# Attention b: periods of a pair, all maxima products of a pair at once in row halves, six shared PSUM banks

## The chip, the cores and the metric

The kernel runs on one core of a Trainium2 chip. The metric is the device time of one execution in microseconds (us); the figure for a kernel is the median of several runs. Differences of under about 0.3% cannot be told from no change.

## What is computed

Two transformer layers on a batch of 2 sequences of 512 tokens, width 512. Each sub-layer is added to the residual stream `x` after a layer norm:

```
x = x + attn_a(ln(x))   # 32 heads of 128, 8 key heads, quantized weights, rope, causal softmax
x = x + ffn(ln(x))      # 8 low-rank experts, the best 2 of 8 by a softmax gate
x = x + attn_b(ln(x))   # 32 query heads of 16, 8 key heads, rope, causal softmax
x = x + ffn(ln(x))
```

The change lies in `attn_b`. For each query head, with q and k of 16 numbers and scale 1/4:

```
att  = einsum('bhgqd,bhkd->bhgqk', q, k) / sqrt(16), masked to k <= q
probs = softmax(att); ctx = einsum('bhgqk,bhkd->bhgqd', probs, v); out = ctx @ Wo
```

## The kernel before

Attention a and the first experts of sequence 0 fill the first part of the time. From about 809 us the kernel is in the loop of attention b, which works on 32 *pairs* (two query heads each, numbered p; `h` is the head in the pair). Two pairs that share a key group position make a *unit* of four heads.

A query or key has 16 numbers, each split in a high and a low part; four combinations of the parts stand in 64 rows (`HALF`), so that float32r products, which run in one pass, come out exact enough. The tiles `qs` (five in rotation, `NQ`) and `ks` have 128 rows: rows 0 to 63 hold the parts, rows 64 and 65 hold the negative row maximum in two parts (in `qs`) against -1 (in `ks`), the rest zeros.

Each pair goes through three kinds of work:

- `maxima` (L742): for the four row tiles of each head, a product of queries and keys into PSUM (`sc_b`, L758, 8 matmuls of 128, 256, 384 or 512 columns over all 128 rows), a masked maximum on VectorE (`DVE`, L762), and the maxima rounded in two parts into `mm` on GpSimd (`POOL`, L770 and L771). It yields three times: tiles 0 and 1, then 3, then 2, each group in two banks.
- `maxima_in` (L776): four transposes of `mm` on TensorE (`tpm`, L781), and two casts on ScalarE (`ACT`, L784) that put the maxima into `qs`.
- `probabilities` (L789): the products again, transposed and with the maximum already subtracted (`st_b`, L805, 8 matmuls in six banks, three yields of two banks), the exponential on ACT (`pT_b`, L811), and the causal cut of the diagonal tiles on POOL (L814). After the second pair of a unit, `weighted_b` (L824) multiplies the four heads' probabilities with the values into one bank (`num_b`, L831; four heads side by side in strips of 32 columns), which ACT copies out (L842). `divided` (L860) and `output_b` (L878) finish the heads.

PSUM has eight banks here: five in `ps_x` for `sc_b`, `st_b` and `tpm` in turn, one in `ps_n` for `num_b`, two in `ps_f` for the side work. The order on TensorE is written out by hand; the tile framework adds the waits. A loop over `total + LEAD` steps (`STEPS` is 3 steps for a pair, `LEAD` is 8) issues in each step one third of a pair's maxima, one third of the probabilities of an earlier pair, now and then `maxima_in`, values that are `due`, and *side work*: experts, the projections of sequence 1, and outputs, taken from generators at a `pace` of us per step. Queries are loaded by `queries_in` (L734), one DMA a pair on the SP queue; as rows 64 and 65 must be zero when the maxima are taken, POOL clears them for each reused tile (L740). `queries_halved` (L724) prepares four pairs at once.

Of the kernel before, what the change touches and what calls it, by code (L numbers as in the profile page):

```python
# [40 lines left out]
def kernel(  # L41
# [21 lines left out]
    nc = tc.nc  # L63
# [6 lines left out]
    x = {}  # L70
# [12 lines left out]
    tri = const.tile([P, S], F32, tag="tri", name="tri")  # L83
# [634 lines left out]
    def keys_in(b, kh):  # L718

        if kh == 0:  # L720
            kparts[b] = spread(khls[b], f"k_{b}", (slice(0, 4, 2), slice(1, 4, 2)))
        nc.sync.dma_start(ks[kh][:HALF], kparts[b][:, ts(kh, 4), :])

    def queries_halved(p):  # L724

        b, kh, g, _ = pairs[p]
        hl = hlp.tile([P, 2, S], F32R, tag="hl", name=f"hl_{p}")
        src = qTs[b][:, kh * 2 + g // 2, :]
        nc.scalar.copy(hl[:, 0, :], src)
        nc.gpsimd.tensor_tensor(hl[:, 1, :], src, hl[:, 0, :].bitcast(F32), ALU.subtract)  # L730
        to = spread(hl, f"q_{p}", (slice(0, 2), slice(2, 4)))
        for n in range(4):
            qparts[p + n] = to

    def queries_in(p):
        _, _, g, pr = pairs[p]
        q = qs[p % NQ]
        nc.sync.dma_start(q[:HALF], qparts.pop(p)[:, ts((g % 2) * 2 + pr, 2), :])
        if p >= NQ:
            nc.gpsimd.memset(q[HALF:HM], 0.0)  # L740

    def maxima():  # L742

        for p, (b, kh, g, pr) in enumerate(pairs):
            q, k = qs[p % NQ].bitcast(F32R), ks[kh].bitcast(F32R)
            top = small.tile([P, NT, 2], F32, tag="top", name=f"top_{p}")
            for tiles in ((0, 1), (3,), (2,)):
                sc = [
                    ps_x.tile([P, S], F32, tag="x", name=f"sc_b_{p}_{tiles[0]}_{h}")
                    for h in range(2)  # L750
                ]
                parts, at = [], 0
                for i in tiles:
                    n = (i + 1) * P
                    parts += [(i, n, h, sc[h][:, at : at + n]) for h in range(2)]
                    at += n
                for i, n, h, part in parts:
                    nc.tensor.matmul(  # L758
                        part, q[:, h, ts(i, P)], k[:, pr * 2 + h, :n], start=True, stop=True
                    )  # L760
                for i, n, h, part in parts:
                    nc.vector.tensor_tensor_reduce(  # L762
                        part, part, tri[:, S - n :], 1.0, -3e38, ALU.add, ALU.max,
                        top[:, i, h : h + 1],
                    )
                if tiles == (2,):
                    mm = mms[p] = mmp[p % len(mmp)]
                    for h in range(2):
                        at = (1 - h) * HALF
                        nc.gpsimd.tensor_copy(mm[:, :, at], top[:, :, h])  # L770
                        nc.gpsimd.tensor_tensor(  # L771
                            mm[:, :, at + 1], top[:, :, h], mm[:, :, at].bitcast(F32), ALU.subtract
                        )
                yield

    def maxima_in(p):  # L776

        mm = mms.pop(p).bitcast(F32)
        tp = ps_x.tile([P, S], F32, tag="x", name=f"tpm_{p}")
        for t in range(NT):  # L780
            nc.tensor.transpose(tp[:HM, ts(t, P)], mm[:, t, :], ident)  # L781
        for h in range(2):
            at = (1 - h) * HALF
            nc.scalar.copy(qs[p % NQ][HALF:HM, h, :].bitcast(F32R), tp[at : at + 2, :])  # L784


    due = []

    def probabilities():  # L789

        for p, (b, kh, g, pr) in enumerate(pairs):
            q, k = qs[p % NQ].bitcast(F32R), ks[kh].bitcast(F32R)
            for tiles in ((0,), (1,), (3, 2)):
                wide = sum(S - j * P for j in tiles)
                for h in range(2):
                    sp = pr * 2 + h
                    st = ps_x.tile([P, S], F32, tag="x", name=f"st_b_{p}_{tiles[0]}_{h}")
                    pT = ptp.tile(
                        [P, wide], F32, tag=f"pT{wide}", name=f"pT_b_{p}_{tiles[0]}_{h}",
                        bufs=5 if wide == S else 8,  # L800
                    )
                    at = 0
                    for j in tiles:
                        n = S - j * P
                        nc.tensor.matmul(  # L805
                            st[:, at : at + n], k[:, sp, ts(j, P)], q[:, h, j * P :],
                            start=True, stop=True,
                        )
                        pTs[b, kh, g, j, sp] = pT[:, at : at + n]
                        at += n  # L810
                    nc.scalar.activation(pT, st[:, :wide], AF.Exp)  # L811

                    diag = pT[:, : len(tiles) * P].rearrange("p (m n) -> p m n", n=P)
                    nc.gpsimd.affine_select(  # L814
                        diag, diag, [[0, len(tiles)], [1, P]], ALU.is_ge, 0.0,
                        base=0, channel_multiplier=-1,
                    )
                if pr == 1:
                    for j in sorted(tiles):
                        pT4 = [pTs.pop((b, kh, g, j, n)) for n in range(4)]  # L820
                        due.append((p * STEPS + LEAD + 2 * (j > 0) + (j > 1), (b, kh, g, j, pT4)))
                yield

    def weighted_b(b, kh, g, j, pT):  # L824
# [1 line left out]

        first, last = j == 0, j == NT - 1
        if first:
            nums[b, kh, g] = ps_n.tile([P, S], F32, tag="num", name=f"num_b_{b}_{kh}_{g}")
        for sp in range(4):  # L830
            nc.tensor.matmul(  # L831
                nums[b, kh, g][ts(sp, STRIP), j * P :], vpads[b][:, j, kh, sp, :], pT[sp],
# [78 lines left out]
    for kh in range(2):  # L911
        keys_in(0, kh)
    queries_halved(0)
    for p in range(2):
        queries_in(p)
    parts(later, 14)

    ms, ps = maxima(), probabilities()
    total = len(pairs) * STEPS
    half = total // 2  # L920
    banks[:] = BESIDE
    side = chain(later, projections(1))
    pace, left = 1.05, 0.0
    for step in range(total + LEAD):
        with tc.manual_schedule(engines={mybir.EngineType.PE}):
            if step == half - 8:
                run(side)
                keys_in(1, 0)
            if step == half - 4:
                side = output_b(0, (0, 1))  # L930
                pace, left = 0.38, 0.0
            if step == half + LEAD:
                keys_in(1, 1)
            if step == half + LEAD + 10:
                side = chain(side, output_b(0, (2, 3)), experts(0, "f2", True))
                pace, left = 1.05, 0.0
            if step == total - 6:
                side = chain(output_b(1, (0, 1)), side)
                pace, left = 1.5, 0.0
            quotients[:] = [q for q in quotients if next(q, None) is not None]  # L940
            p, at = divmod(step + 4, STEPS)
            if at == 0 and p % 4 == 3 and p + 1 < len(pairs):
                queries_halved(p + 1)
            if at == 0 and 2 <= p < len(pairs):
                queries_in(p)
            p, at = divmod(step - 4, STEPS)
            if at == 0 and 0 <= p < len(pairs):
                maxima_in(p)
            if LEAD <= step:
                next(ps)  # L950
            if step < total:
                next(ms)

            if len(due) > 1 and due[1][0] <= step:
                for _ in range(2):
                    weighted_b(*due.pop(0)[1])
            left += pace
            while left > 0:
                got = next(side, None)
                if got is None:  # L960
                    left = 0.0
                else:
                    left -= got
    banks[:] = ALONE
    while due:
        weighted_b(*due.pop(0)[1])
# [95 lines left out]
```

## Time and profile before

| what | us |
|---|---|
| median of 3 runs (1113.66 to 1117.13) | 1114.39 |
| the profiled execution's own time | 1118.06 |
| its span, first to last instruction | 1116.3 |
| loop of attention b, first `sc_b` to last `num_b` (809.4 to 1055.3) | 246 |
| of it with much side work (839.4 to 892.3), seven pairs | 52.9 |
| of it with little side work (892.3 to 959.0), ten pairs | 66.7 |
| after the loop, to the end | 61 |

The granted TensorE clock was 0.992 of full speed over the span. All durations of single instructions come from that one profiled execution. TensorE's instructions overlap in the profile, so that the time one of them takes is best read from the start of one to the start of the next. A float32 product appears as two matmuls, a float32r product as one.

### The profile page before, as it was taken

How to read it: one execution, taken by the hardware profiler on the slowest of the kernel's cores; microseconds unless marked ns; L12 is line 12 of the kernel's file. 1: busy time of each engine (PE TensorE's matmuls, PEld its weight loads, DVE VectorE, ACT ScalarE, POOL GpSimd, SP SyncE). 2: the span in 40 equal slices, each digit the busy share in tenths (PEclk: the TensorE clock that was granted, in tenths of full speed). 3: DMA queues.
4: the chain of work that ended last, by engine and by line, in shares of the span. 5: the costliest groups of instructions: out<-in, count | busy, mean ns of one | idle time of the engine just before them, and what ended most of it. 6: DMA issues, size and time to landing. Idle time of an engine off the chain costs nothing.

```text
span 1116.3 us, 16200 instructions
## 1 busy us (share of the span) xinstructions
PE 1060.7 (95%) x4940; PEld 708.8 (63%) x4940; DVE 880.8 (79%) x2195; ACT 617.4 (55%) x1421; POOL 587.4 (53%) x920
## 2 busy tenths in 40 slices
PE   5799999999999999999999999999989989999988
PEld 3467677777777777777777777546457555555543
DVE  6889899999999999999999889574376677877252
ACT  3556566577566566566565665513157566585410
POOL 2557566666656656756756666261245566454200
PEclk9999999999999999999999999999989999999999
DMA  7301011022010010010021000042342235111000
GB/s 288 114 1 38 1 38 38 1 76 68 9 39 24 15 38 14 26 38 8 32 76 38 1 1 1 1 156 63 91 156 77 61 106 152 44 44 26 10 33 38
DMA packets 21030, 58.11 MB, mean 52 GB/s; under 512 B 3152, under 2 KB 4112, under 8 KB 18128
## 3 DMA queue, kind: packets, MB, share of 16 engines
q1 hardware_dynamic: 20944, 57.08, 15.6%
q8 instruction: 40, 0.66, 0.2%
q14 instruction: 46, 0.38, 0.1%
HBM read 43.30 MB, written 12.58 MB: 50 GB/s over the span
## 4 chain that ended last, share of the span: by engine, by line
PE 80%; DVE 10%; ACT 3%; POOL 3%; issue 2%; DMA 1%; SPq 0%; ACTq 0%; DVEq 0%; POOLq 0%
PE av L429 11%; PE sc L396 11%; PE tp L424 5%; PE ps_o L439 5%; PE ps_o L438 5%; PE ps_q L358 5%; PE ph_f L207 5%; PE ps_q L359 5%; PE num_b L831 3%; PE st_b L805 3%; PE py_f L266 3%; PE sc_b L758 3%; PE pq_b L678 2%; PE po L885 2%; DVE r_q L365 2%
## 5 line engine op out<-in xcount | busy, mean ns | idle before, releaser
L404 ACT ACTIVATE p<-sc,nmx 128x128 f32<-128x128 f32 (+3 forms) x256 | 135.7, 530 | 95.1 <-DVE nmx L399 92.1
L376 POOL TENSOR_TENSOR r_q<-r_q,tab 128x512 f32<-128x512 f32 x64 | 82.5, 1289 | 190.2 <-DVE rs_q L375 190.2
L396 PE MATMUL sc<-kT,qT 128*128 128x128 f32 (+3 forms) x512 | 180.0, 433 | 1.2 <-POOL qT L377 0.9
L365 DVE SCALAR_TENSOR_TENSOR r_q<-ps_q,s_q,r_q 128x512 f32<-128x512 f32 x192 | 143.4, 747 | 36.1 <-PE ps_q L359 22.4
L413 POOL TENSOR_SCALAR p<-p,rden 128x128 f32<-128x128 f32 (+3 forms) x256 | 140.3, 562 | 58.5 <-DVE rden L411 24.5
L425 ACT COPY pT<-tp 128x128 f32<-128x128 f32 (+3 forms) x256 | 109.4, 428 | 104.1 <-PE tp L424 103.5
L762 DVE CUSTOM_DVE_ANT_0 sc_b<-sc_b,tri 128x128 f32<-128x128 f32 (+3 forms) x256 | 119.6, 516 | 47.3 <-PE sc_b L758 42.5
L429 PE MATMUL av<-pT,v 128*128 128x512 f32 (+3 forms) x512 | 148.5, 433 | 0.0
L429 PEld LDWEIGHTS av<-pT,v 128*128 128x128 f32 x512 | 97.0, 190 | 80.2 <-issue 53.9
L448 DVE SCALAR_TENSOR_TENSOR acc<-ps_o,s_o,acc 128x512 f32<-128x512 f32 x186 | 137.3, 738 | 5.5 <-PE ps_o L439 5.4
L399 DVE CUSTOM_DVE_ANT_0 sc<-sc,tri 128x128 f32<-128x128 f32 (+3 forms) x256 | 125.1, 489 | 8.1 <-PE sc L396 7.3
L358 PE MATMUL ps_q<-xh,w_q 128*128 128x512 f32 x256 | 122.7, 479 | 7.6 <-DVE r_q L365 7.6
L424 PE MATMUL tp<-ident,p 128*128 128x128 f32 x640 | 112.9, 272 | 2.6 <-POOL p L413 2.6
L396 PEld LDWEIGHTS sc<-kT,qT 128*128 128x128 f32 x512 | 95.6, 189 | 25.3 <-ACT p L404 2.0
L438 PE MATMUL ps_o<-ah,w_o 128*128 128x512 f32 x256 | 107.9, 422 | 1.7 <-DVE acc L448 1.0
L811 ACT ACTIVATE pT_b<-st_b 128x384 f32<-128x384 f32 (+1 forms) x192 | 90.1, 528 | 34.4 <-PE st_b L805 33.5
L439 PE MATMUL ps_o<-al,w_o 128*128 128x512 f32 x256 | 104.8, 410 | 3.5 <-DVE al L152 3.5
L424 PEld LDWEIGHTS tp<-ident,p 128*128 128x128 f32 x640 | 83.0, 141 | 30.7 <-issue 6.4
L359 PE MATMUL ps_q<-xl,w_q 128*128 128x512 f32 x256 | 101.2, 395 | 0.0
L814 POOL TENSOR_SCALAR_AFFINE_SELECT pT_b<-pT_b 128x128 f32<-128x128 f32 (+1 forms) x192 | 62.2, 333 | 64.7 <-ACT pT_b L811 62.2
L377 POOL TENSOR_TENSOR qT<-r_q,rs_q 128x512 f32<-128x512 f32 x64 | 85.5, 1335 | 1.0
L446 POOL TENSOR_TENSOR acc<-acc,part 128x512 f32<-128x512 f32 x62 | 79.9, 1288 | 10.2 <-ACT part L445 10.1
(182 smaller groups left out, 2065.4 us busy)
## 6 DMA issues: line engine op xcount, KB each, us to landing
codes_q<-in_q_codes_dram SPq DMA_DIRECT2D x8, 1024.0 KB
codes_o<-in_o_codes_dram SPq DMA_DIRECT2D x8, 1024.0 KB
spread_q<-hl SPq DMA_DIRECT2D x16, 512.0 KB
qs<-spread_q SPq DMA_DIRECT2D x32, 256.0 KB
x_a<-in_x_dram SPq DMA_DIRECT2D x8, 256.0 KB
codes_k<-in_k_codes_dram SPq DMA_DIRECT2D x2, 1024.0 KB
codes_v<-in_v_codes_dram SPq DMA_DIRECT2D x2, 1024.0 KB
x_r<-in_x_dram SPq DMA_DIRECT2D x8, 256.0 KB
```

The costliest lines, as they stand in the source:

```text
L358: nc.tensor.matmul(ps, w[:, c, ts(h, A_HD)], xh[b][:, c, :], start=True, stop=False)
L359: nc.tensor.matmul(ps, w[:, c, ts(h, A_HD)], xl[b][:, c, :], start=False, stop=True)
L365: nc.vector.scalar_tensor_tensor(r, ps, s, r, ALU.mult, ALU.add)
L396: nc.tensor.matmul(sc[:, :n], qT[:, ts(i, P)], kT[:, :n], start=True, stop=True)
L399: nc.vector.tensor_tensor_reduce(sc[:, :n], sc[:, :n], tri[:, S - n :], -(A_HD**-0.5), 3e38, ALU.add, ALU.min, nmx,)
L404: nc.scalar.activation(pr, sc[:, :n], AF.Exp, bias=nmx, scale=-1.0, accum_out=den[:, i % 2 : i % 2 + 1],)
L413: nc.gpsimd.tensor_scalar(prs[j], prs[j], rden[:, j % 2 : j % 2 + 1], 1.0, ALU.mult, ALU.mult)
L424: nc.tensor.transpose(tp[:, j, :], prs[i][:, ts(j, P)], ident)
L429: nc.tensor.matmul(av[:, j * P :], v[:, j, :], pT[:, j, j * P :], start=(j == 0), stop=(j == NT - 1))
L438: nc.tensor.matmul(ps, w[:, h, ts(n, P)], ah, start=True, stop=False)
L439: nc.tensor.matmul(ps, w[:, h, ts(n, P)], al, start=False, stop=True)
L448: nc.vector.scalar_tensor_tensor(to, ps, s, to, ALU.mult, ALU.add)
```

## The change

A pair's three steps become one *period*. In each period, in TensorE's order: values of a finished unit (all 16 products, four tiles by four heads, in one go), then all eight maxima products of pair n into six banks, then side work and the three parts of the probabilities of pair n-2 in turn, with `maxima_in` of pair n-1 ahead of the third part. The maxima products read 64 rows only: head 0 of a pair stands in rows 0 to 63, head 1 in rows 64 to 127, each with its maxima in the first two rows of the other half. POOL no longer clears rows; queries and keys come with two DMAs of half the size. The bank of `num_b` joins the others: six in one pool.

```diff
-        nc.gpsimd.memset(pad[HALF:HM], -1.0)
+        for sp in range(4):
+            at = (1 - sp % 2) * HALF
+            nc.gpsimd.memset(pad[at : at + 2, sp, :], -1.0)
...
-    ps_x = ctx.enter_context(tc.tile_pool(name="ps_x", bufs=5, space=PSUM))
-    ps_n = ctx.enter_context(tc.tile_pool(name="ps_n", bufs=1, space=PSUM))
+    ps_x = ctx.enter_context(tc.tile_pool(name="ps_x", bufs=6, space=PSUM))
...
-    STEPS, LEAD = 3, 8
+    LEAD = 2
...
-        nc.sync.dma_start(ks[kh][:HALF], kparts[b][:, ts(kh, 4), :])
+        for h in range(2):
+            nc.sync.dma_start(
+                ks[kh][ts(h, HALF), h : 4 : 2, :], kparts[b][:, kh * 4 + h : kh * 4 + 4 : 2, :]
+            )
...
-        q = qs[p % NQ]
-        nc.sync.dma_start(q[:HALF], qparts.pop(p)[:, ts((g % 2) * 2 + pr, 2), :])
-        if p >= NQ:
-            nc.gpsimd.memset(q[HALF:HM], 0.0)
+        of = qparts.pop(p)
+        for h in range(2):
+            nc.sync.dma_start(qs[p % NQ][ts(h, HALF), h, :], of[:, (g % 2) * 4 + pr * 2 + h, :])
...
+            two, three, one = (
+                [ps_x.tile([P, S], F32, tag="x", name=f"sc_b_{p}_{i}_{h}") for h in range(2)]
+                for i in (2, 3, 1)
+            )
+            parts = []
+            for i in (2, 0, 3, 1):
+                n = (i + 1) * P
+                for h in range(2):
+                    part = (two[h][:, 384:], one[h][:, :n], two[h][:, :n], three[h])[i]
+                    parts.append((i, n, h, part))
+                    rows = ts(h, HALF)
                     nc.tensor.matmul(
-                        part, q[:, h, ts(i, P)], k[:, pr * 2 + h, :n], start=True, stop=True
+                        part, q[rows, h, ts(i, P)], k[rows, pr * 2 + h, :n], start=True, stop=True
                     )
...
-                        due.append((p * STEPS + LEAD + 2 * (j > 0) + (j > 1), (b, kh, g, j, pT4)))
+                        due.append((p + LEAD + 1, (b, kh, g, j, pT4)))
...
-            nums[b, kh, g] = ps_n.tile([P, S], F32, tag="num", name=f"num_b_{b}_{kh}_{g}")
+            nums[b, kh, g] = ps_x.tile([P, S], F32, tag="x", name=f"num_b_{b}_{kh}_{g}")
...
-    pace, left = 1.05, 0.0
-    for step in range(total + LEAD):
+    pace, left = 3.2, 0.0
...
+    for n in range(total + LEAD + 1):
...
+            for _ in range(3):
+                quotients[:] = [q for q in quotients if next(q, None) is not None]
+            if n % 4 == 1 and n + 3 < total:
+                queries_halved(n + 3)
+            if 0 < n and n + 2 < total:
+                queries_in(n + 2)
+            fill(0.1)
...
+            while due and due[0][0] <= n:
+                weighted_b(*due.pop(0)[1])
+            if n < total:
                 next(ms)
+            for part in range(3):
+                fill((0.5, 0.2, 0.2)[part])
+                if part == 2 and 1 <= n <= total:
+                    maxima_in(n - 1)
+                if LEAD <= n < total + LEAD:
+                    next(ps)
```

`fill(share)` takes side work worth that share of the pace. The paces of the later stages become 1.2, 3.2 and 4.5 us a period where they were 0.38, 1.05 and 1.5 us a step, and the stages begin at the same pairs as before.

More of the change, by code (lines that the diff above doesn't have):

```diff
@@ L746, in maxima @@
             top = small.tile([P, NT, 2], F32, tag="top", name=f"top_{p}")
[L747 to L757, printed above, removed]
+            two, three, one = (
+                [ps_x.tile([P, S], F32, tag="x", name=f"sc_b_{p}_{i}_{h}") for h in range(2)]
+                for i in (2, 3, 1)
+            )
@@ L760, in maxima @@
                     )
[L761 to L773, printed above, removed]
@@ L774, in maxima @@
-                yield
+            for i, n, h, part in parts:
+                nc.vector.tensor_tensor_reduce(
+                    part, part, tri[:, S - n :], 1.0, -3e38, ALU.add, ALU.max, top[:, i, h : h + 1]
+                )
+            mm = mms[p] = mmp[p % len(mmp)]
+            for h in range(2):
+                at = (1 - h) * HALF
+                nc.gpsimd.tensor_copy(mm[:, :, at], top[:, :, h])
+                nc.gpsimd.tensor_tensor(
+                    mm[:, :, at + 1], top[:, :, h], mm[:, :, at].bitcast(F32), ALU.subtract
+                )
@@ L776, in maxima_in @@
+            yield
     def maxima_in(p):
@@ L782, in maxima_in @@
         for h in range(2):
-            at = (1 - h) * HALF
-            nc.scalar.copy(qs[p % NQ][HALF:HM, h, :].bitcast(F32R), tp[at : at + 2, :])
+            rows = slice((1 - h) * HALF, (1 - h) * HALF + 2)
+            nc.scalar.copy(qs[p % NQ][rows, h, :].bitcast(F32R), tp[rows, :])
     due = []
@@ L913 @@
     queries_halved(0)
-    for p in range(2):
+    for p in range(3):
         queries_in(p)
@@ L918 @@
     ms, ps = maxima(), probabilities()
-    total = len(pairs) * STEPS
+    total = len(pairs)
     half = total // 2
@@ L922, with fill @@
     side = chain(later, projections(1))
-    pace, left = 1.05, 0.0
-    for step in range(total + LEAD):
+    pace, left = 3.2, 0.0
+    def fill(share):
+        nonlocal left
+        left += pace * share
+        while left > 0:
+            got = next(side, None)
+            if got is None:
+                left = 0.0
+            else:
+                left -= got
+    for n in range(total + LEAD + 1):
         with tc.manual_schedule(engines={mybir.EngineType.PE}):
-            if step == half - 8:
+            if n == half - 3:
@@ L927 @@
                 run(side)
                 keys_in(1, 0)
-            if step == half - 4:
+            if n == half - 1:
                 side = output_b(0, (0, 1))
-                pace, left = 0.38, 0.0
-            if step == half + LEAD:
+                pace, left = 1.2, 0.0
+            if n == half + LEAD:
                 keys_in(1, 1)
-            if step == half + LEAD + 10:
+            if n == half + LEAD + 4:
                 side = chain(side, output_b(0, (2, 3)), experts(0, "f2", True))
-                pace, left = 1.05, 0.0
@@ L937 @@
-            if step == total - 6:
+                pace, left = 3.2, 0.0
+            if n == total - 2:
                 side = chain(output_b(1, (0, 1)), side)
[L939 to L951, printed above, removed]
-                next(ms)
[L954 to L963, printed above, removed]
+                pace, left = 4.5, 0.0
```

## The prediction, made before the change was run

> **What bounds the kernel now.** I read the page first, then the busy time by stage, then the timeline of the loop of attention b.
>
> ```profile
> span 1116.3 us, 16200 instructions
> ...
> PE 1060.7 (95%) x4940; PEld 708.8 (63%) x4940; DVE 880.8 (79%) x2195; ACT 617.4 (55%) x1421; POOL 587.4 (53%) x920
> ...
> PE av L429 11%; PE sc L396 11%; PE tp L424 5%; PE ps_o L439 5%; PE ps_o L438 5%; PE ps_q L358 5%; PE ph_f L207 5%; PE ps_q L359 5%; PE num_b L831 3%; PE st_b L805 3%; PE py_f L266 3%; PE sc_b L758 3%; PE pq_b L678 2%; PE po L885 2%; DVE r_q L365 2%
> ```
>
> TensorE is busy 95% of the span and carries 80% of the chain that ended last; but the lines of attention b (num_b, st_b, sc_b) are only 3% each, so a change there moves per cents at most. By stage:
>
> ```profile
> core 0: us, PE busy (x) PEld busy (x) DVE busy (x) ACT busy (x) POOL busy (x), PEclk, DMA share, GB/s
> ...
> 839.40:892.30 52.90, 52.20 (x314) 34.28 (x314) 35.76 (x139) 32.75 (x75) 30.37 (x85) 1.00 0.25 71
> 892.30:959.00 66.70, 58.89 (x386) 34.88 (x384) 50.39 (x181) 44.78 (x92) 41.45 (x113) 1.00 0.38 116
> ```
>
> In the first stretch (seven pairs, much side work, 7.55 us a pair) TensorE is busy 52.2 of 52.9 us and nothing else is near: it bounds. In the second (ten pairs, little side work, 6.67 us a pair) TensorE is busy 58.9 of 66.7 us and no engine is full: waits bound. In the timeline the time of TensorE's work is read from start to start:
>
> ```profile
> 859.74 0.51 PE L758 MATMUL sc_b<-ks,qs 128*128 128x384 f32 x2
> 860.09 1.02 PE L678 MATMUL pq_b<-wq,xnT_b 128*128 128x512 f32 x2
> ...
> 861.29 0.62 PE L758 MATMUL sc_b<-ks,qs 128*128 128x128 f32 x4
> 861.75 1.02 PE L678 MATMUL pq_b<-wq,xnT_b 128*128 128x512 f32 x2
> 862.61 0.60 PE L781 MATMUL tpm<-ident,mm 128*66 128x128 f32 x4
> 862.97 0.70 PE L805 MATMUL st_b<-qs,ks 128*128 128x128 f32 x4
> 863.51 0.63 PE L758 MATMUL sc_b<-ks,qs 128*128 128x512 f32 x2
> 864.07 1.71 PE L831 MATMUL num_b<-pT_b,vpad 128*32 128x512 f32 x16
> 865.71 1.12 PE L678 MATMUL pq_b<-wq,xnT_b 128*128 128x512 f32 x2
> ```
>
> The maxima's products of a pair (L758) take 0.35 us (384 columns twice), 0.46 (128 and 256 twice) and 0.47 (512 twice; the 0.56 shown to the values holds a switch): 1.28 us. The transposes tpm take 0.44 with their tail, a pair's L805 as much as its maxima, 1.28. The first half of a unit's values takes 1.64 us; the second, in the same view, 0.79 (867.58 to 868.37). As single matmuls of 512 columns there start every 0.43 us, four strips together, the eight passes should take 2.13: 0.15 us per group goes into entering and leaving the strips. A busy period is thus 1.28 + 1.28 + 0.44 + 2.43/2 + side work 3.13 = 7.34, against 7.55 measured; only 0.2 us a pair is waiting.
>
> What happens behind the third part of the probabilities is in the timeline of all engines:
>
> ```profile
> 914.62 0.63 PE L781 MATMUL tpm<-ident,mm 128*66 128x128 f32 x4
> ...
> 915.01 0.70 PE L805 MATMUL st_b<-qs,ks 128*128 128x128 f32 x4
> 915.29 1.17 ACT L784 CAST qs<-tpm 2x512 fp32r<-2x512 f32 x2 [0.48 <-PE tpm L781]
> ...
> 915.55 0.83 PE L758 MATMUL sc_b<-ks,qs 128*128 128x512 f32 x2
> ...
> 916.48 0.87 ACT L811 ACTIVATE pT_b<-st_b 128x384 f32<-128x384 f32 x2
> ...
> 917.10 0.77 POOL L814 TENSOR_SCALAR_AFFINE_SELECT pT_b<-pT_b 128x256 f32<-128x256 f32 x2 [0.32 <-ACT pT_b L811]
> ```
>
> E, the moment when TensorE is done with that part, is 915.55, where the next product starts. ACT has the two casts of the maxima in front of the exponentials, so these end at E+1.36 and E+1.80 (917.35), and POOL's cut of the second at E+2.32 (917.87). The waits over the loop:
>
> ```profile
> POOL qs L740 <- PE st_b L805: 25.3, 26, 1.8
> ...
> PEld tpm L781 <- POOL mm L771: 14.3, 16, 2.1
> ...
> PE tpm L781 <- POOL mm L771: 7.0, 8, 1.9
> ```
>
> TensorE waits 21 us for mm before the transposes, most of it with little side work; POOL's clearing stands in the same queue and itself waits 25 us for L805.
>
> **The change, part by part.** Products in row halves: a pair's 8 products of 1.28 us become four pairs of neighbours, each in its own half. No row of before is in row halves. Bounds: 1.28 us if the halves run one after another, 0.64 if they run together. The nearest row is the values' strips, where four matmuls start 7 ns apart; I take 0.64 and keep 1.28 for the range. Two more switches a pair at 0.075 each (half of the 0.15 above), but one group of values instead of two a unit, 0.15 back.
>
> A rule of the Trainium skill speaks against it: "TensorEngine Tiling (Array Packing)", PSUM Bottleneck, says that tiling speeds up TensorE and not the emptying of PSUM. Here the maxima's reductions start 0.24, 0.38, 0.49 and 0.62 us apart for the four widths (timeline at 906.5 to 912.3), 3.46 us a pair on DVE. By the rule the saved 0.64 would be lost in all 32 periods (plus 20 us against a sum that counts it). By the trace DVE was busy 35.8 of 52.9 us in the busy stretch, so it is won there and lost only where side work is scarce. I follow the trace.
>
> The border of two periods: this is the new wait. Six maxima banks of six can't be had until the probabilities' banks are empty. In turn, tile 2 and 0 take banks of the first and second part (free), tile 3 the second's and that of tpm, tile 1 the two of the third part, which ACT frees at E+1.4 and E+1.85. TensorE works in order, so everything written behind the eight products waits.
> - A period without values: 0.3 us of side work, products, wait for the last bank, last product: TensorE is free at E+2.05, where it would be at E+0.94. Then side work 2.83, L805 1.28, tpm 0.44: period 6.60.
> - A period with values: 0.3 side, the first two tiles' values 1.6 (E+1.9), then the wait for POOL's cut (E+2.4), 0.65 more, products; the last takes the bank of num_b, which ACT copies 0.35 us later in 0.6: TensorE is free at E+4.3, not E+3.2. With 4.55 behind it: 8.85.
> The mean is 7.73 against 7.55: +0.18 for some 15 busy periods (pairs 4 to 11, 22, 23 and 26 to 30), +2.7 us. The gain of 0.64 and of the waits for mm is there, but 1.1 us a period is waited.
>
> Little side work (ten periods): now the chain is DVE's. Without values: the first reduction starts at E+0.5 (0.3 from a product's start to DVE's, as at 911.37 and 911.74), 3.46 us of them free the last bank at E+4.1, and tpm's end and the third part's second half behind it set the next E at E+4.85. With values the products start at E+3.15 and everything is 3.2 later: E+8.05. Mean 6.45. Two sets of divisions fall here (reciprocals 2 x 1.74, shuffles 2 x 0.75, products 2 x 0.69 = 6.4 us of DVE each) and four additions of 0.68; the 3 us in which DVE now idles during the values take most, I charge 6 us. 64.5 + 6 = 70.5 against 66.7: +4 us. The waits for mm are gone in this figure, since tpm comes a period later.
>
> At nothing: POOL loses 27 clearings of 0.945 us (25.5 us and 25.3 waited), hidden before by ACT's exponentials, which POOL still waits for; if that cover were gone it would be a gain. SP issues 64 DMAs of queries for 32 (0.47 us each: +15 us on SP over the loop) and 8 for 4 of keys; SP is idle most of the time, and queries are now asked for two periods (13 us) ahead of use, before 1.33 pairs (9 us); the spread's DMAs in front of them in SP's queue still come a period earlier. If that cover failed, the products of a pair would be late by the difference. The eight short memsets of -1 replace two of 2.0 us at 747 us, 29 us ahead of the keys. Side work is the same in sum and in its stages, 35 periods for 34.7. The last values stand inside the loop with 4 us of side work behind them; the end from 1055 us on is left at 61 us.
>
> Sum: 2.7 + 4 = +6.7 us on a profiled execution of 1118.1 us, which is 3.7 above the median; on the median of 1114.4 I put +6: 1120.
>
> **The rivals.**
> - Faster: the border waits don't come, since ACT does the exponentials ahead of the casts, or the side work at the border covers them. For: ACT is busy under 70% of either stretch; its order isn't written by hand. Against: in the chain above the casts come first, being ready first. Then the busy periods are 7.73 - 1.1 + 0.3 = 6.9 (-0.65, times 15: -10), little side work about -3 (values' wait gone): -13, 1101.
> - Even: TensorE waits half of that at the border: busy periods 7.2 (-5), the rest +2 to +4: within 3 us of before, 1113.
> - Slower by one mechanism: the row halves do not run together, or each switch drains for as long as a product. Where values are due, 0.64 more per pair then lies on the path (without values it is hidden in the wait for the banks): 16 x 0.64 = +10 on top of +6: 1130. It decides from about 0.2 us per pair. For it: no row of before shows such a product, and a switch to strips costs. Against: the strips run together.
> - It does not do what it says: if all six banks at once make DVE the chain even in busy periods (the skill's rule), the lead of DVE there, 1.7 us by my times (tpm's bank is free at E+4.0 and asked for at E+5.7), must be gone; side work on DVE of more than that in a period does it. +20 - 6 of the waits it covers: about 1134.
>
> **How the numbers follow.** Forecast (+2 to +12) 0.40; faster rival 0.29; even 0.14; slower rivals 0.17. The range from 1102 to 1136 leaves out the ends of the first and the last, 2 in 10; cases of both signs hold the chance, and the likeliest one's own range is 1116 to 1127. A measurement tells some 0.3% (3.3 us) from no change: faster by more 0.31 (the faster rival and 0.02 of the even case), within 0.14 (0.12 of the even case, 0.02 of the forecast), slower 0.55 (0.38 of the forecast and the slower rivals).
>
> **What would show it.** Right: L758 starts in pairs some 10 ns apart; waits of L758 for ACT pT_b and of num_b for POOL pT_b, in sum over 15 us; no L740, tpm's wait for mm near 0; periods alternate near 6.6 and 8.9 us with side work, 4.9 and 8 without. Wrong: L758 starts 0.2 us apart (no overlap); periods under 7.2 with side work (no border wait); a wait for queries' DMAs; or a change outside 809 to 1056 us.

## The result, and the profile after

The changed kernel takes 1132.86 us (median of 4 runs, 1131.32 to 1134.67), the kernel before 1115.62 in the same runs: a ratio of 1.0151, with a 95% interval of 1.0138 to 1.0165. It is slower by 1.5%, 17 us, where 6 us were forecast. That lies in the stated range of 1102 to 1136 us, but outside the forecast's own range of 1116 to 1127: only the slower rivals hold it. In the text below a difference between two kernels in us is the difference of their ratios to before, times 1115.6.

The page of the kernel after, its span, the busy times and the granted clock:

```profile
span 1133.0 us, 16209 instructions
...
PE 1070.4 (94%) x4940; PEld 709.7 (63%) x4940; DVE 873.8 (77%) x2195; ACT 614.1 (54%) x1421; POOL 564.2 (50%) x899
...
PEclk9899999999999999999999999999989999989999
```

TensorE has the same 4940 products, and although the maxima's products were to be cheaper it is busy 10 us longer. POOL lost the 23 us of clearing and nothing came of it. Of the three 8s in the row PEclk (a slice is 28.3 us), the first lies ahead of the loop and the second stands in the row of before too:

```profile
PEclk9999999999999999999999999999989999999999
```

New in the loop is the third, from 991 to 1020 us. The profiled execution has a mean clock of 0.982, before it was 0.992.

The busy time by stage, first of before, then of after (columns: stretch, length, busy time of each engine, PEclk, DMA share, GB/s). The stretches are the same pairs in both: 4 to 12, 12 to 22 and 22 to 31, each from first maxima product to first maxima product:

```profile
832.00:892.30 60.30, 59.38 (x378) 38.93 (x377) 39.67 (x155) 38.53 (x87) 34.70 (x98) 1.00 0.29 84
892.30:959.00 66.70, 58.89 (x386) 34.88 (x384) 50.39 (x181) 44.78 (x92) 41.45 (x113) 1.00 0.38 116
959.00:1027.70 68.70, 66.22 (x413) 39.11 (x413) 52.10 (x196) 44.37 (x87) 33.47 (x105) 1.00 0.13 36
```

```profile
836.50:903.70 67.20, 63.41 (x382) 39.06 (x382) 42.77 (x164) 37.87 (x86) 27.76 (x89) 1.00 0.22 60
903.70:971.80 68.10, 61.64 (x385) 35.17 (x384) 45.31 (x173) 44.00 (x90) 31.59 (x105) 0.95 0.38 113
971.80:1049.00 77.20, 69.28 (x384) 39.84 (x380) 50.99 (x192) 42.69 (x86) 25.00 (x90) 0.91 0.13 30
```

The loss lies in the two stretches with much side work (+6.9 and +8.5 us), not in the one without (+1.4). In the first of them TensorE filled 59.38 of 60.30 us before; now 3.8 us are empty, and much of the rest is "busy" with instructions that wait for an operand. The clock rows say 0.95 of 68.10 us and 0.91 of 77.20: as the clock records of these traces hold only the two steps full and half, that is 6.8 and 13.7 us at half speed. Before: none.

To tell work from waiting I took the starts of TensorE's products, charged each with its time at full clock (for `sc_b` half of it where row halves are used), and put the rest of the way to the next start down to the product that came late. This is a count of mine, not a view of the profile: with other times at full clock the late times shift, so that their growth says more than their size. What the halves fall short of half the time, and what the half clock costs, is in it too:

| pairs | length before, after | late before, after | of it `sc_b` | side work | `st_b` | half clock after |
|---|---|---|---|---|---|---|
| 4 to 12 | 60.3, 67.2 | 7.1, 18.1 | 1.9, 7.0 | 2.0, 7.5 | 0.8, 1.2 | 0 |
| 12 to 22 | 66.7, 68.1 | 21.6, 25.8 | 8.6, 10.2 | 0.7, 1.9 | 5.2, 9.0 | 6.8 |
| 22 to 31 | 68.7, 77.2 | 13.6, 24.6 | 5.2, 6.8 | 2.3, 8.5 | 3.2, 6.9 | 13.7 |

The first four pairs take 3.2 us more, the rest after pair 31 takes 5.0 less, the loop starts 1.3 later, and the end is 61.5 for 61.1. Late time grows by 26 us in the three stretches: at the maxima (`sc_b`), as forecast, but more at the side work, and in the two later stretches at `st_b`.

The border of two periods, the forecast's new wait, in the timeline of all engines after (start, duration, what; in brackets the idle time ahead of it and who ended it). E is 860.98:

```profile
860.63 0.58 ACT L787 CAST qs<-tpm 2x512 fp32r<-2x512 f32 x1 [0.17 <-PE tpm L784]
...
860.98 0.79 PE L763 MATMUL sc_b<-ks,qs 64*128 64x384 f32 x5
...
861.43 0.57 ACT L787 CAST qs<-tpm 2x512 fp32r<-2x512 f32 x1
...
861.91 0.85 ACT L814 ACTIVATE pT_b<-st_b 128x384 f32<-128x384 f32 x2
...
862.06 1.14 PE L763 MATMUL sc_b<-ks,qs 64*128 64x512 f32 x3 [0.29 <-ACT qs L787]
...
863.12 1.12 PE L680 MATMUL pq_b<-wq,xnT_b 128*128 128x512 f32 x2
```

Five products run, the sixth waits for the bank that ACT's second cast reads, the last two for the banks of the exponentials, and TensorE is free at E+2.14. The prediction had E+2.05. With values (E 849.86, free 853.84) it is E+3.98, predicted 4.3.

What the forecast did not have is in the periods with side work. First one with projections, in pairs 4 to 12:

```profile
856.53 0.46 DVE L767 CUSTOM_DVE_ANT_0 sc_b<-sc_b,tri 128x256 f32<-128x256 f32 x1
...
857.38 0.28 DVE L152 TENSOR_TENSOR khl<-tpk,khl 128x128 fp32r<-128x128 f32 x1
...
857.71 1.13 PE L653 MATMUL pkv_b<-wkv,xnT_b 128*128 128x256 f32 x4 [1.30 <-DVE khl L152]
```

DVE is at its eight reductions until 856.91, and only then come the operations of the projection (L618, L620, L152) that stood behind them; TensorE's next product waits 1.30 us for the last. In these pairs four waits of side products are listed, 3.2 us in sum: 1.3 for DVE, 1.1 for POOL and 0.8 for ACT, which both work on what DVE made. In the same pairs of before none is listed. Then one with outputs:

```profile
1037.24 0.57 DVE L767 CUSTOM_DVE_ANT_0 sc_b<-sc_b,tri 128x384 f32<-128x384 f32 x1 [3.44 <-PE sc_b L763]
...
1037.62 1.13 PE L888 MATMUL po<-wo,oN_b 128*128 128x512 f32 x2
...
1040.41 0.46 DVE L767 CUSTOM_DVE_ANT_0 sc_b<-sc_b,tri 128x256 f32<-128x256 f32 x1
...
1040.80 0.68 DVE L892 TENSOR_TENSOR x_r<-x_r,po 128x512 f32<-128x512 f32 x1
...
1041.53 1.32 PE L888 MATMUL po<-wo,oN_b 128*128 128x512 f32 x2 [2.78 <-DVE x_r L892]
...
1042.09 1.62 PE L808 MATMUL st_b<-qs,ks 128*128 128x512 f32 x2
...
1043.32 1.08 ACT L814 ACTIVATE pT_b<-st_b 128x512 f32<-128x512 f32 x2 [6.06 <-PE st_b L808]
```

The first output product ends at 1038.75, but the addition that empties its bank stands in DVE's queue behind all eight reductions, which run from 1037.24 to 1040.80. The next output product waits 2.78 us, `st_b` stands behind it on TensorE, and ACT waits 6.06 us for `st_b`. The waits of the loop, TensorE's products and its weight loads (sum, times, longest):

```profile
PE st_b L808 <- DVE top L767: 6.6, 11, 1.9
PE sc_b L763 <- ACT qs L787: 3.2, 8, 0.7
...
PE po L888 <- DVE x_r L892: 3.0, 2, 2.8
```

```profile
PEld st_b L808 <- DVE top L767: 17.8, 38, 2.1
PEld sc_b L763 <- ACT qs L787: 8.7, 14, 1.0
...
PEld sc_b L763 <- ACT pT_b L814: 5.1, 26, 0.2
...
PEld num_b L834 <- POOL pT_b L817: 3.4, 13, 0.4
```

The largest is `st_b` waiting for a bank that a reduction on DVE still reads: 17.8 us of late weight loads, where before had 5.3:

```profile
PEld st_b L805 <- DVE top L762: 5.3, 17, 0.6
```

By stretch, in the order of the table, it is 2.3, 5.7 and 6.5 us, before 0.2, 2.3 and 2.2. So a good part of it lies where little was lost, and in pairs 4 to 12 the side work's waits weigh more. The waits for `mm` are gone, as forecast.

### The profile page after: what moved, and what is told of

The parts are those of the page before. It is cut to its first block, busy times and chain, and to the rows that moved or that the text cites. A ratio compares the mean times of both kernels' runs of the same rounds, so it can differ in the third digit from the quotient of the medians.

```text
span 1133.0 us, 16209 instructions
## 1 busy us (share of the span) xinstructions
PE 1070.4 (94%) x4940; PEld 709.7 (63%) x4940; DVE 873.8 (77%) x2195; ACT 614.1 (54%) x1421; POOL 564.2 (50%) x899
## 5 line engine op out<-in xcount | busy, mean ns | idle before, releaser
L365 DVE SCALAR_TENSOR_TENSOR r_q<-ps_q,s_q,r_q 128x512 f32<-128x512 f32 x192 | 143.5, 747 | 36.9 <-PE ps_q L359 23.2
L767 DVE CUSTOM_DVE_ANT_0 sc_b<-sc_b,tri 128x384 f32<-128x384 f32 (+3 forms) x256 | 116.4, 525 | 60.3 <-PE sc_b L763 28.4
L808 PE MATMUL st_b<-qs,ks 128*128 128x256 f32 (+3 forms) x256 | 79.1, 415 | 9.0 <-DVE top L767 6.6
```

Of the source, the lines that this page charges most:

```text
L365: nc.vector.scalar_tensor_tensor(r, ps, s, r, ALU.mult, ALU.add)
L767: nc.vector.tensor_tensor_reduce(part, part, tri[:, S - n :], 1.0, -3e38, ALU.add, ALU.max, top[:, i, h : h + 1])
```

## The experiments

**1. Each half of the change alone.** `e1_halves_only` is before with the queries and keys in row halves (tiles, DMAs, casts and products of the change); `e2_periods_only` is after with products over all 128 rows, for which POOL clears the rows again.

```diff
 # e1, against before; e2 does the reverse to after
-                        part, q[:, h, ts(i, P)], k[:, pr * 2 + h, :n], start=True, stop=True
+                        part, q[rows, h, ts(i, P)], k[rows, pr * 2 + h, :n], start=True, stop=True
```

> The kernel before with the row halves alone (layout, split DMAs, no clearing); steps, banks and order stay. Theory A (the loss is the waits at the border of periods, the products themselves win): faster than before, by 0.64 less two or three pairs of switches (0.15 each) for some 20 pairs where TensorE bounds, and by part of the 21 us that the transposes wait for mm, as the clearing is gone from POOL: 1100 to 1108 us. Theory B (the loss is the switches into and out of row halves): slower than before, over 1120 us.

> The changed kernel with the maxima's products over all 128 rows again (and POOL clearing the four rows as before); periods, six banks and order stay. Theory A (border waits): slower than the changed kernel by up to 0.64 us in the periods with values, less in the others, where the wait for the banks hides it: 1136 to 1146 us. Theory B (switches cost more than the halves win): as fast as the changed kernel or faster, 1120 to 1133 us.

Measured: e1 1127.29 us, ratio 1.0091 (1.0072 to 1.011); e2 1133.15 us, ratio 1.0152 (1.0132 to 1.0172). In the row halves theory A fell and B, the switches, held: alone they cost 10 us. In the periods A fell too; they alone cost all of the 17 us, and halves on top of them change nothing. The two halves of the change don't add.

The trace of e1 shows what row halves are worth there (start, duration):

```profile
860.17 0.44 PE L763 MATMUL sc_b<-ks,qs 64*128 64x384 f32 x2
860.54 1.13 PE L680 MATMUL pq_b<-wq,xnT_b 128*128 128x512 f32 x2
861.11 0.91 PE L810 MATMUL st_b<-qs,ks 128*128 128x384 f32 x2
861.94 0.50 PE L763 MATMUL sc_b<-ks,qs 64*128 64x128 f32 x4
862.37 1.13 PE L680 MATMUL pq_b<-wq,xnT_b 128*128 128x512 f32 x2
```

From the first product to what follows it is 0.37 and 0.43 us, where the same two groups took 0.35 and 0.46 before. The two heads do start together (3 ns apart in the trace of after, 1049.007 and 1049.010), and two products of 384 columns, which took 0.35 us one after the other, should then take 0.18; the other 0.2 us goes into leaving the halves. Entering them costs too. The line of before that stands ahead of its 861.29 (shown with the prediction):

```profile
860.54 0.91 PE L805 MATMUL st_b<-qs,ks 128*128 128x384 f32 x2
```

From the probabilities' products to the maxima's it is 0.75 us before and 0.83 in e1; the other two groups of that pair enter 0.07 and 0.09 us later. So the halves make a pair 0.1 to 0.2 us dearer, an estimate of 3 to 6 us over 32 pairs. In pairs 4 to 12, where the clock is full in both, e1 takes 62.8 us and before 60.3. The rest of the 10 us may be the clock's, which comes next.

In one block the halves save what was forecast, if nothing waits. From after, a block of the first pairs, then one with values:

```profile
815.80 0.90 PE L763 MATMUL sc_b<-ks,qs 64*128 64x384 f32 x8
816.63 1.98 PE L266 MATMUL py_f<-lora_b,hT_f 128*128 128x512 f32 x4
...
852.72 1.18 PE L763 MATMUL sc_b<-ks,qs 64*128 64x384 f32 x8
...
853.52 0.18 PEld L763 LDWEIGHTS sc_b<-ks,qs 64*128 64x128 f32 x1 [0.22 <-ACT o_b L845]
...
853.84 1.99 PE L653 MATMUL pkv_b<-wkv,xnT_b 128*128 128x256 f32 x8
```

The first takes 0.83 us, as do the few blocks without a wait in e3, e5, e6 and e7 (0.83 or 0.84); where nothing waits over whole rows, the eight take 1.37 to 1.39 in e2. In the second the eighth weight load waits for ACT's copy of `num_b`, whose bank its product takes. So it is in the blocks with values: behind that first one, the twelve shortest blocks of after take 1.05 to 1.11 us, all with the eighth weight load waiting for ACT, and save about 0.29 us instead of 0.55. Without values the banks hold the block for 1.93 us or more, with halves (after) and without (e2) alike.

The clock by stage, first e1, then e2:

```profile
900.00:960.00 60.00, 54.73 (x338) 28.28 (x336) 41.90 (x153) 36.76 (x78) 28.16 (x93) 0.94 0.38 120
960.00:1010.00 50.00, 48.02 (x254) 25.13 (x253) 31.09 (x114) 30.26 (x60) 16.18 (x60) 0.83 0.14 38
```

```profile
903.00:972.00 69.00, 62.65 (x386) 38.15 (x386) 45.30 (x176) 43.95 (x90) 41.47 (x125) 1.00 0.35 112
972.00:1049.00 77.00, 68.86 (x381) 41.01 (x380) 51.91 (x195) 42.78 (x86) 32.67 (x106) 0.98 0.11 30
```

With row halves the clock falls to half for some 24 us behind the first pairs in e1 (0.06 of 60 and 0.17 of 50 us, twice) and 20.5 in after; with whole rows in e2 for 3.4, and in no trace with whole rows for longer (before, e8 and the variants of before in 3 and 6: none or 3.4). The mean clock of every run says the same: 0.981 to 0.986 in e1 and 0.982 to 0.985 in after, 0.989 to 0.993 in e2. My starts put the products' own loss at 9 us in after, an estimate. In e2 POOL's clearing returns in front of the cuts, and the wait of `num_b` for POOL grows from 3.4 to 10.8 us (weight loads). So in the periods row halves win 0.29 us in every second pair and POOL's clearing, and about as much is lost again, probably to the clock; the fourth experiment tries it.

**2. The border wait.** `e3_casts_behind` puts the casts behind the exponentials (`maxima_in` after the third part); `e4_tile1_later` does the two products of tile 1, which took the last banks, ahead of the second part of the probabilities.

```diff
 # e3
-                if part == 2 and 1 <= n <= total:
-                    maxima_in(n - 1)
                 if LEAD <= n < total + LEAD:
                     next(ps)
+                if part == 2 and 1 <= n <= total:
+                    maxima_in(n - 1)
```

```diff
 # e4
-            for i in (2, 0, 3, 1):
+            for tiles in ((2, 0, 3), (1,)):
...
+                if tiles == (2, 0, 3):
+                    yield
...
+                if part == 1 and n < total:
+                    next(ms)
```

> The changed kernel with the transposes and casts of the maxima issued behind the third part of the probabilities, so that ACT takes the two exponentials first and the casts (1.16 us) after. Theory A (border: values and the last maxima products wait for ACT's exponentials of the third part): 0.3 to 1.0 us less per period, 1105 to 1125 us. Theory C (the loss is the block of eight reductions on DVE, which holds up the side work's operations and the probabilities' banks): within 4 us of the changed kernel, 1129 to 1137 us.

> The changed kernel with tile 1's two products (of eight) moved from the border to just ahead of the second part of the probabilities: at the border four banks are enough, and the last two products no longer wait for the exponentials of the third part; one more pair of switches a period. Theory A (border): 0.5 to 1 us less per period against 0.15 for the switches, 1108 to 1124 us. Theory C (block of reductions on DVE): within 4 us of the changed kernel or slower, 1129 to 1140 us.

Measured: e3 1130.99 us, ratio 1.013 (1.011 to 1.0151): within 3 us of after, so theory A missed and C held. The values' products did come earlier (late time at `num_b` between pairs 12 and 22: 3.9 to 1.4 us, and less in the other stretches), but the weight loads of `st_b` waited 20.4 us for DVE where after had 17.8. What was late next was DVE. e4 1124.99 us, ratio 1.0073 (1.0053 to 1.0092), 9 us better than after, just above the upper end of A. It takes the wait for the exponentials' banks off the border, but it also lets DVE have its work in two pieces; it doesn't tell the two theories apart.

**3. DVE's reductions.** `e5_fill_even` moves side work from before the first part to between the others. `e6_short_reductions` and `b6_short_reductions` reduce only the last 128 columns of each tile, in after and in before.

```diff
 # e5
-                fill((0.5, 0.2, 0.2)[part])
+                fill(0.3)
 # e6 and b6
+                part = part[:, n - P :]
                 nc.vector.tensor_tensor_reduce(
-                    part, part, tri[:, S - n :], 1.0, -3e38, ALU.add, ALU.max, top[:, i, h : h + 1]
+                    part, part, tri[:, S - P :], 1.0, -3e38, ALU.add, ALU.max, top[:, i, h : h + 1]
```

> The changed kernel with the side work in three even shares of 0.3 ahead of the three parts of the probabilities, where it was 0.5, 0.2 and 0.2. Theory C1 (TensorE waits in the side work because several units of it stand in a row, each waiting for DVE, ACT or POOL to finish the one before): 3 to 8 us less, 1125 to 1130 us, idle time at side instructions down by a third. Theory C2 (it waits because DVE is busy with the eight reductions when the side work's turn comes): no gain, 1131 to 1136 us, as the first part of the probabilities then comes earlier and waits for the reductions instead.

> The changed kernel with each maximum taken over the last 128 columns of its tile alone (the other columns are left out of the maximum), so that the eight reductions of a pair take about 1.9 us of DVE for 3.5; products, banks and order stay. Theory C2 (the block of reductions holds up the probabilities' banks and the side work): most of the 24 us of waits of the probabilities for DVE and part of the side work's go, 1108 to 1122 us. Theory A (only the border waits for ACT count): 1128 to 1134 us.

> The kernel before with each maximum over the last 128 columns of its tile alone (the other columns are left out of the maximum), as a control: the same cut in the changed kernel gave 20 us. If DVE's reductions are what the change brought onto the path: 0 to 8 us less than before, 1108 to 1116 us. If they were on the path before as much: 15 to 22 us less, 1094 to 1101 us.

Measured: e5 1136.68 us, ratio 1.0192 (1.0171 to 1.0212), 5 us slower than after, so C1 fell and C2 held but for 1 us: with less side work ahead of the first part `st_b` comes to the reductions sooner and waits for them longer (23.9 us of late loads). e6 1113.35 us, ratio 0.9981 (0.9973 to 0.999): 19 us less than after. b6 1105.3 us, ratio 0.9912 (0.9895 to 0.9929): 10 us less than before, between what the theories gave. The same cut is worth twice as much in the changed kernel. (The 24 us in the expectation of e6 add the 6.6 of products to the 17.8 of weight loads; they are nearly all the same waits, 18.1 us in the trace.) In e6 the waits read:

```profile
PE sc_b L763 <- ACT qs L788: 5.0, 10, 0.7
PE st_b L809 <- DVE top L768: 2.9, 6, 0.7
```

`st_b` waits 2.9 us for DVE instead of 6.6, and among the late weight loads that wait is no longer one of the seven largest. Beyond the start the loop has no half clock in e6 either, though it uses row halves; its mean clock is 0.990 to 0.998. So the halves alone don't set it off; what else it takes was not settled. (e4, with halves and 9 us faster than after, has 20.5 us of it.)

**4. Does the half clock set the time?** `e7_whole_rows_midway` is after with whole rows for pairs 12 to 28 (and POOL's clearing for them), where the clock had fallen.

```diff
-                    rows = ts(h, HALF)
+                    rows = slice(0, P) if 12 <= p < 29 else ts(h, HALF)
```

> The changed kernel with the maxima's products of pairs 12 to 28 over all 128 rows (POOL clears their four rows), the others in row halves. Theory D (row halves let the TensorE clock fall to half where little side work is at hand: 20 us at half clock behind pair 12 in the profile): granted clock 0.99 for 0.982, no half clock between pairs 12 and 29, and 3 to 8 us less though the products are longer, 1125 to 1130 us. Without that theory: clock unchanged, 2 to 6 us more, 1135 to 1139 us.

Measured: 1135.11 us, ratio 1.0175 (1.0158 to 1.0192), not faster. The half clock between pairs 12 and 31 fell from 20.5 to 3.4 us, so the halves bring it about; but that stretch became only 1.8 us shorter (143.5 for 145.3), while pairs 4 to 12 and the end, where nothing was edited, came out 1.7 and 2.9 us longer in this execution, the end with 6.8 us at half clock that after does not have there. Theory D is right about the clock and wrong about the time. Of what the clock gives back, the longer products take an estimate of 2.6 us (0.29 us in the nine pairs with values); how much POOL's clearing takes, and how much was never on the path, is not shown.

**5. All at once, or in thirds.** `e8_thirds_whole_rows` is e2 with the maxima in three pieces: tiles 2 and 0 at the border, tile 3 ahead of the first part, tile 1 ahead of the second.

```diff
-            for i in (2, 0, 3, 1):
+            for tiles in ((2, 0), (3,), (1,)):
...
+                if tiles != (1,):
+                    yield
...
+                if part < 2 and n < total:
+                    next(ms)
```

> Periods as in the changed kernel, but the maxima's products over all 128 rows and in thirds again: tiles 2 and 0 at the border, tile 3 ahead of the first part of the probabilities, tile 1 ahead of the second. Values in one go, six shared banks and the late transposes stay. Theory E (the loss is that all eight products stand at one place: TensorE waits for six free banks there, and DVE gets its 3.5 us of reductions in one block with nothing before it): back near the kernel before, 1112 to 1120 us. Theory F (the loss is the values in one go at the border, or the shared sixth bank): as slow as the changed kernel, 1129 to 1136 us.

Measured: 1118.78 us, ratio 1.0024 (1.0011 to 1.0037), as theory E had it: 14 us less than e2, with the same rows, banks and periods. Its timeline on TensorE:

```profile
870.70 0.71 PE L767 MATMUL sc_b<-ks,qs 128*128 128x512 f32 x2
871.24 0.63 PE L814 MATMUL st_b<-qs,ks 128*128 128x512 f32 x2
871.71 1.03 PE L680 MATMUL pq_b<-wq,xnT_b 128*128 128x512 f32 x2
872.18 0.80 PE L767 MATMUL sc_b<-ks,qs 128*128 128x256 f32 x2
```

Nothing in these lines waits. Side work is late by 1.5 us in pairs 4 to 12, where before had 2.0 and e2 5.2; that stretch is 62.4 us long, e2's 68.9. The thirds undo two things at once, the wait for six banks at the border and DVE's block of reductions. That the second weighs more follows from e3, which eased the border and gained 2 us, and e6, which shortened the reductions, left the border as it was and gained 19; no run parts them cleanly.

**6. What was there to win.** `b0_tpm_later` is before with the transposes one step later, which takes away the wait for `mm` alone; `b1_six_banks` is before with the bank of `num_b` in the common pool; `b2_six_banks_tpm_later` is both.

```diff
 # b0
-            p, at = divmod(step - 4, STEPS)
+            p, at = divmod(step - 5, STEPS)
 # b1
-    ps_x = ctx.enter_context(tc.tile_pool(name="ps_x", bufs=5, space=PSUM))
-    ps_n = ctx.enter_context(tc.tile_pool(name="ps_n", bufs=1, space=PSUM))
+    ps_x = ctx.enter_context(tc.tile_pool(name="ps_x", bufs=6, space=PSUM))
...
-            nums[b, kh, g] = ps_n.tile([P, S], F32, tag="num", name=f"num_b_{b}_{kh}_{g}")
+            nums[b, kh, g] = ps_x.tile([P, S], F32, tag="x", name=f"num_b_{b}_{kh}_{g}")
```

> The kernel before with the transposes of the maxima one step later (nothing else). They wait 21 us for POOL's mm in the kernel before. If those waits are on the path, 4 to 12 us less, 1104 to 1112 us; if the wait of one step only passes on to DVE and ACT behind it, within 3 us of before, 1113 to 1119 us.

> The kernel before with the values' bank shared with the other five (six in one pool) and nothing else. Theory F (the shared bank costs): over 1120 us. Otherwise within 4 us of before, 1112 to 1119 us; a bank more for the products where no values are open could give 1 to 3 us.

> The kernel before with six shared banks and the transposes of the maxima one step later (their 21 us of waits for POOL's mm go). Each was run alone: the banks gave 0.3%, the later transposes nothing. If the sixth bank lets DVE and ACT use the time that the transposes no longer wait: 2 to 5 us less than with the banks alone, 1107 to 1111 us. If the wait only passes on behind them again: as with the banks alone, 1111 to 1114 us.

Measured: b0 1115.85 us, ratio 0.9996 (0.9986 to 1.0006); b1 1112.67 us, 0.9972 (0.9962 to 0.9983); b2 1108.4 us, 0.9928 (0.9915 to 0.9942). The waits of b0, products and then weight loads, and the last line for b2:

```profile
PE sc_b L758 <- ACT pT_b L811: 4.5, 12, 0.9
...
PE tpm L781 <- POOL mm L771: 1.2, 2, 0.6
```

```profile
PEld sc_b L758 <- ACT pT_b L811: 10.8, 24, 1.1
```

```profile
PEld sc_b L757 <- ACT pT_b L810: 4.6, 14, 1.1
```

(The 21 us in the expectations add 7.0 of the products to 14.3 of the weight loads ahead of them; in the trace the 7.0 lie inside the 14.3.) In b0 the 7.0 us that products waited for `mm` are down to 1.2, the 14.3 us of weight loads are no longer among the largest, and the time is the same: the next product waits for the exponentials' banks instead (10.8 us of loads; before, where it isn't among the nine largest, at most 3.6). With the sixth bank that wait is 4.6, and now the later transposes pay. So theory F fell: the shared bank costs nothing, it gives 0.3%. b2 is the best version that takes the whole maximum: 0.7% faster than before, 2.2% faster than the change.

## Why the prediction was right in sign and short in size

- *Range*: the 17 us lie in it by the rivals; the forecast's own case stopped at 1127.
- *Border wait*: right. Free at E+2.14 and E+3.98 against 2.05 and 4.3 predicted. Which wait it is was named only in part: POOL's cut and the exponentials' banks show 3.4 and 5.1 us of late loads, not over 15; the casts' bank shows 8.7.
- *Alternating periods*: right for little side work: 4.84 us on average without values and 8.78 with, predicted 4.85 and 8.05 ahead of 6 us charged to the stretch for divisions; it takes 68.1 us, predicted 70.5, with 6.8 us at half clock that no term had. Wrong with much: from pair 5 the intervals with values average 10.20 us, those without 6.97, predicted 8.85 and 6.60.
- *Busy periods, the step that failed*: "+2.7" us for 15 periods; the two stretches that hold them grew by 15.4. The 0.2 us of waiting a pair that was read before is low too: the count above has 7.1 us in eight pairs. The lead of 1.7 us that DVE was to have was counted for the transposes' bank alone. Side work also needs DVE: its evictions (L892, and the projections' L152, L618 and L620) stand behind 3.5 us of reductions in DVE's order, and TensorE, in order too, holds `st_b` behind the side work. The rule of "TensorEngine Tiling (Array Packing)", PSUM Bottleneck, in the Trainium skill, that tiling speeds up TensorE and not the emptying of PSUM, was set aside because DVE was busy 35.8 of 52.9 us. For the halves it came true: after is as slow as e2. But the 17 us are not the tiling's, as e2 loses them over whole rows; 14 of them come of the order (e8), about which the mean said nothing: with a DVE busy 42.8 of 67.2 us TensorE still waited. The shorter reductions (19 us gained in after, 10 in before) and the thirds (14 us gained) show it, the thirds together with the border's banks.
- *Row halves*: right in size, wrong in worth. The block was to take 0.64 and two switches of 0.075, 0.79 in all, and took 0.83 where nothing waits. But with values its eighth product waits for the bank of `num_b`, which leaves 0.29 of the 0.64, and without values the banks hide the rest. The half clock wasn't in the sum at all.
- *Waits for mm gone*: right, and worth nothing by itself (b0). They were not 21 us but 14.3, as the 7.0 of the products lie inside the weight loads' waits.
- *At nothing*: the end (61.5 us) and the place of the change were right; the loop's first four pairs were missed by 3.2 us, and the last stretch, 5.0 us shorter, wasn't counted. POOL's clearing was hidden in before, as assumed, but not in the periods, where e2 has it in front of the cuts.
- *The rivals*: of the two slower ones, 1134 by DVE in busy periods was nearest in time and in mechanism; 1130 by the row halves was right that they pay little and that switches cost (e1), wrong that they run one after another.

Open: how much of the half clock lies on the path. The products lose an estimated 9 us to it in after; in e7 the stretch gave back 1.8. Nor was it tried why the clock falls where it does. The Trainium skill, "TensorE: Matmul & The Clock Gate", Part 1, lets TensorE's recent activity set the gate. By the profile's busy share TensorE was as active in after (69.28 of 77.20 us) as in e2 (68.86 of 77.00), so this share doesn't tell why; the window of about 3.4 us that the section gives is seen here only in that the slow times in after are 3.4 or 10.2 us long.

## What to carry to other kernels

When all products of a stage are gathered in one place, the engine that empties PSUM gets its work in one lump, and whatever else it does for TensorE stands behind the lump: look at the order in its queue, not at its share of busy time. A wait that the profile lists is worth something only if what would end next is earlier: look for the next releaser before you count it, and don't add the wait of a product to that of its own weight load. A cheaper product should be priced with its switches, and the granted clock looked at when products in row halves come in.

## What the runs showed of the hardware

Products in row halves of 64 rows start 3 ns apart and do run together: a block of eight in which nothing waits takes 0.83 us for 1.38 over whole rows. Leaving the halves takes some 0.2 us and entering them 0.07 to 0.09 us more than whole rows, so that a group of two gains nothing (0.37 us for 0.35). And in a loop where no listed wait of a product on TensorE is over 2.8 us (after), the clock fell to half for up to 10.2 us at a time, with row halves (20.5 us in after, some 24 in e1) and nearly not with the same products over all rows (3.4 us in e2).
